# A graph network's convolutions: row products first, the constant row last in each bank, one product for both constants

## The chip, the cores and the metric

The kernel runs on one core of a Trainium2 chip, as one program. The metric is the device time of an execution in microseconds (us); lower is better. A core has five engines that work side by side: TensorE (PE) for matrix products, VectorE (DVE), ScalarE (ACT) and GpSimd (POOL) for work on tiles, SyncE (SP) for transfers. TensorE writes into PSUM, eight banks of 128 partitions x 512 fp32 numbers; the other tiles lie in SBUF.

## The reference, cut to what matters

Sixteen graphs (B) of 1024 nodes (N) with 128 features (D) pass four blocks: a graph network with dilated neighbourhoods, an attention, a graph attention and a graph convolution. The change is in the first block alone, after the dilation has thinned each adjacency:

```python
def _sage(x, adj, Wr, Wx, b, mf):
    deg = jnp.clip(jnp.sum(adj, axis=-1, keepdims=True), 1.0, None)
    agg = jnp.einsum('bij,bjd->bid', adj, x) / deg
    out = agg @ Wr + x @ Wx + b
    nrm = jnp.maximum(jnp.linalg.norm(out, axis=-1, keepdims=True), NORM_EPS)
    return out / nrm * mf[..., None]

def _bn(x, g, b):
    m = jnp.mean(x, axis=(0, 1))
    v = jnp.var(x, axis=(0, 1))
    return (x - m) * jax.lax.rsqrt(v + BN_EPS) * g + b

h1 = _bn(jax.nn.relu(_sage(x, adj_d, Wr1, Wx1, b1, mf)), g1, be1)
h2 = _bn(jax.nn.relu(_sage(h1, adj_d, Wr2, Wx2, b2, mf)), g2, be2)
h3 = _bn(jax.nn.relu(_sage(h2, adj_d, Wr3, Wx3, b3, mf)), g3, be3)
xc = jnp.concatenate([h1, h2, h3], axis=-1) * mf[..., None]
return (xc @ Wl + bl) * mf[..., None]
```

A batch normalization runs over all nodes of all graphs, so the statistics of a layer are complete only after its last graph.

## The kernel before, in words

The program has four stages: the dilation, the convolutions (`convolutions_plain`, in the profile from about 690 to 1611 us), the attentions, and a check whose fallback does not run. Only the convolutions matter here.

**Normalization folded into the next layer.** Instead of normalizing h, the kernel keeps the ReLU's output as it is. With `scale` and `shift` of the normalization, the next layer's weights become weight x scale per input feature (L1144), and the shift becomes a constant row: bias + shift @ Wx for every node, and shift @ Wr for those nodes that have a neighbour at all. `through` (L1129) makes both products of the shift with the unscaled weights; `row_parts` (L1007) splits the resulting 6 x 128 row into three bf16 parts, rows 0 to 2 for the first sum and 3 to 5 for the second. In L1143 the weights are scaled in place, after `through` has read them. `final` keeps the share of the last linear layer (`wl`, L1146 to L1148).

**One layer, per graph b.** A half graph (512 nodes) fills one PSUM bank, tile `o`, from a pool of four banks: two graphs. In it lie four blocks of 128 nodes. For a bank TensorE runs, in the text's order:

- L1087: the constant rows 0 to 2 for all four blocks at once, 3 rows of ones against a row that is repeated four times, 512 columns, bf16. It starts the bank's accumulation.
- L1091, layers 1 and 2: per block, the six rows of the constant against `has` (L1083). `has` is a 6 x 1024 bf16 tile made by VectorE from `rdeg`, one over the degree or zero, that is compared with `floor` per row: `floor` is 2 in rows 0 to 2, which no `rdeg` exceeds, so these rows of `has` are 0, and 0 in rows 3 to 5, so these are 1 where a node has neighbours. The tile has two buffers.
- L1093 and L1094: per block, the row products, aggT x Wr and hT x Wx, 128 x 128 fp32 (each appears as two records).

Then the chain of a graph: squares (L1099, ScalarE), sums over features (L1100, VectorE), a maximum (L1102), a power for the inverse root (L1045, GpSimd), eight scaled ReLUs (L1106, ScalarE). In layers 0 and 1 `neighbours` follows: transposes (L1029), copies to hT (L1030), a split of h into three bf16 parts (L676 to L679), 48 products g with the adjacency C (L1040), and the division by the degree into aggT (L1042). In layer 2 only transposes (L1114) and copies (L1115). Either way hT is spilled to memory (L1116) and its statistics are taken (L1118).

**The change of layer.** After the last graph: `bn_aggr` (L1120), the power for `scale` (L1123), `scale` times gamma (L1124), `shift` (L1126, L1127), the small products of `through`, `row` (L1141), `row_parts`, the scaling of both weights, the product of the shift with `wl`.

**Order.** Each engine works through its own queue in order. In this stage the queues are not in the text's order: a scheduler that knows each instruction's inputs and the free buffers fills waits of one graph with work of another. In the trace, for example, transposes of one graph stand between row products of another. In the attentions the order is written out by hand, with costs and due times; the diff doesn't touch it.

Of the kernel before, what the change touches and what calls it, by code (L numbers as in the profile page):

```python
# [6 lines left out]
F32 = mybir.dt.float32  # L7
# [5 lines left out]
ALU = mybir.AluOpType  # L13
# [4 lines left out]
B, N, D = 16, 1024, 128  # L18
P = 128
NB = N // P  # L20
H, HD = 4, 32
HN = N // 2
# [21 lines left out]
def flat(ap):  # L44
    return ap.rearrange("p a b -> p (a b)")
# [916 lines left out]
def convolutions_plain(tc, x, ident, ap, xp, h0, minus_half, kept, rdeg, spill, final, Wr, Wx, bias, gamma, beta, Wl, bl):  # L962
    nc = tc.nc
    with ExitStack() as ctx:
        cp = ctx.enter_context(tc.tile_pool(name="c_const", bufs=1))
# [9 lines left out]
        ones16 = cp.tile([3, P], BF16, name="ones16")  # L975
        nc.vector.memset(ones16, 1.0)

        floor = cp.tile([6, 1], F32, name="floor")
        nc.vector.reduce_sum(floor, ident[0:6, 0:3], axis=AX.X)
        nc.vector.tensor_scalar(floor, floor, 2.0, None, op0=ALU.mult)  # L980

        def matrix(w, name):
            t = cp.tile([P, D], F32, name=name)
            nc.sync.dma_start(t, w)
            return t

        def column(v, name):
            t = cp.tile([P, 1], F32, name=name)
            with nc.allow_non_contiguous_dma(reason="128 values, once"):
                nc.sync.dma_start(t, v[:, None])  # L990
            return t
# [8 lines left out]
        hT = [kp.tile([P, N], F32, name=f"hT{b}") for b in range(B)]  # L1000
        aggT = [kp.tile([P, N], F32, name=f"aggT{b}") for b in range(B)]
# [5 lines left out]
        def row_parts(rows, name):  # L1007

            left = small.tile([6, D], F32, name="left")
            nc.vector.tensor_copy(left, rows)  # L1010
            t = cp.tile([6, D], BF16, name=name)
            nc.vector.memset(t, 0.0)
            for k in range(3):
                part = small.tile([6, D], BF16, name="part")
                nc.vector.tensor_copy(part, left)
                nc.vector.tensor_tensor(left, left, part, op=ALU.subtract)
                nc.vector.scalar_tensor_tensor(t, part, pick[:, k:k + 1], t, op0=ALU.mult, op1=ALU.add)
            return t
# [25 lines left out]
        def rsqrt(out, v):  # L1044
            nc.gpsimd.tensor_tensor(out, v, minus_half[:, :v.shape[-1]], op=ALU.pow)  # L1045

        for b in range(B):
# [16 lines left out]
            if b == 1:  # L1064
                wr = [matrix(w, f"wr{i}") for i, w in enumerate(Wr)]
                wx = [matrix(w, f"wx{i}") for i, w in enumerate(Wx)]
# [4 lines left out]
                bet = [column(v, f"bet{i}") for i, v in enumerate(beta)]  # L1071
# [3 lines left out]
        wr_s, wx_s, constant = wr[0], wx[0], row_parts(b6[0], "const0")  # L1075
        for l in range(3):
            stats = kp.tile([P, 2 * B, 6], F32, name="stats")
            for b in range(B):
                if l:
                    rd6 = xp.tile([6, N], F32, name="xt")  # L1080
                    nc.sync.dma_start(rd6, rdeg[b][None, :].to_broadcast([6, N]))
                    has = w2.tile([6, N], BF16, name="has")
                    nc.vector.tensor_scalar(has, rd6, floor, None, op0=ALU.is_gt)  # L1083
                ps = []
                for hf in range(2):
                    t = pso.tile([P, HN], F32, name="o")
                    nc.tensor.matmul(t, ones16, constant[0:3, None, :].to_broadcast([3, 4, D]), start=True, stop=False)  # L1087
                    blocks = [(t[:, c * P:(c + 1) * P], slice((4 * hf + c) * P, (4 * hf + c + 1) * P)) for c in range(4)]
                    if l:
                        for o, rows in blocks:  # L1090
                            nc.tensor.matmul(o, has[:, rows], constant, start=False, stop=False)  # L1091
                    for o, rows in blocks:
                        nc.tensor.matmul(o, aggT[b][:, rows], wr_s, start=False, stop=False)  # L1093
                        nc.tensor.matmul(o, hT[b][:, rows], wx_s, start=False, stop=rows.stop % HN == 0)  # L1094
                    ps.append(t)
                nrm = small.tile([P, 2, NB], F32, name="nrm")
                for hf in range(2):
                    sq = w2.tile([P, 4, D], F32, name="sq")
                    nc.scalar.activation(flat(sq), ps[hf], AF.Square)  # L1099
                    nc.vector.reduce_sum(nrm[:, 0, 4 * hf:4 * hf + 4], sq, axis=AX.X)  # L1100

                nc.vector.tensor_scalar(nrm[:, 0, :], nrm[:, 0, :], 1e-24, None, op0=ALU.max)  # L1102
                rsqrt(nrm[:, 1, :], nrm[:, 0, :])
                h = w2.tile([P, NB, D], F32, name="h")
                for c in range(NB):
                    nc.scalar.activation(h[:, c, :], ps[c // 4][:, c % 4 * P:(c % 4 + 1) * P], AF.Relu,  # L1106
                                         scale=nrm[:, 1, c:c + 1])
                if l < 2:
                    neighbours(b, h)
                else:  # L1110
                    for hf in range(2):
                        t = pst.tile([P, HN], F32, name="t")
                        for c in range(4):
                            nc.tensor.transpose(t[:, c * P:(c + 1) * P], h[:, 4 * hf + c, :], ident)  # L1114
                        nc.scalar.copy(hT[b][:, hf * HN:(hf + 1) * HN], t)  # L1115
                nc.scalar.dma_start(spill[l, b], hT[b])  # L1116
                for hf in range(2):
                    nc.vector.bn_stats(stats[:, 2 * b + hf, :], hT[b][:, hf * HN:(hf + 1) * HN])  # L1118
            mv = small.tile([P, 2], F32, name="mv")
            nc.vector.bn_aggr(mv, stats.rearrange("p n s -> p (n s)"))  # L1120
            nc.vector.tensor_scalar(mv[:, 1:2], mv[:, 1:2], BN_EPS, None, op0=ALU.add)
            scale = cp.tile([P, 1], F32, name=f"scale{l}")
            rsqrt(scale, mv[:, 1:2])  # L1123
            nc.vector.tensor_tensor(scale, scale, gam[l], op=ALU.mult)  # L1124
            shift = cp.tile([P, 1], F32, name=f"shift{l}")
            nc.vector.tensor_tensor(shift, mv[:, 0:1], scale, op=ALU.mult)  # L1126
            nc.vector.tensor_tensor(shift, bet[l], shift, op=ALU.subtract)  # L1127

            def through(w, out, part):  # L1129
                six = small.tile([P, 6], F32, name="six")  # L1130
                nc.vector.memset(six, 0.0)
                nc.vector.tensor_copy(six[:, part], shift.to_broadcast([P, 3]))
                nc.tensor.matmul(out, six, w, start=part.start == 0, stop=part.stop == 6)

            if l < 2:
                wr_s, wx_s = wr[l + 1], wx[l + 1]
                ps = pst.tile([6, D], F32, name="t")
                through(wx_s, ps, slice(0, 3))
                through(wr_s, ps, slice(3, 6))
                row = small.tile([6, D], F32, name="row")  # L1140
                nc.vector.tensor_tensor(row, b6[l + 1], ps, op=ALU.add)  # L1141
                constant = row_parts(row, f"const{l + 1}")
                for w in (wr_s, wx_s):  # L1143
                    nc.vector.tensor_scalar(w, w, scale, None, op0=ALU.mult)  # L1144
            ps = pst.tile([3, D], F32, name="t")
            nc.tensor.matmul(ps, shift.to_broadcast([P, 3]), wl[l], start=True, stop=True)  # L1146
            nc.vector.tensor_tensor(last[0:3], last[0:3], ps, op=ALU.add)
            nc.vector.tensor_scalar(wl[l], wl[l], scale, None, op0=ALU.mult)  # L1148
# [671 lines left out]
```

## Time and profile before

| what | us |
|---|---|
| times of the runs | 4033.46, 4037.02, 4050.93 (median 4037.02) |
| the profiled execution | 4039.04 |
| its span in the profile | 4037.30 |
| TensorE busy over the span | 3474.4 (86%) |
| VectorE, ScalarE, GpSimd busy | 2527.9, 2401.7, 794.7 |
| layer 0 and the first neighbours' sums until its change of layer | from about 690 to 1160.5 |
| layer 1 | 1160.5 to 1458.5 |
| layer 2 and the last constants | 1458.5 to 1611.5 |
| L1087, 96 times | 384 ns median |
| L1091, 256 times | 214 ns median |

How to read it: the profile lists, per engine, each instruction with its start, its length, its line in the code, its output and inputs, and in brackets how long the engine was idle before it and whom it waited for. Neighbouring instructions of one kind are merged ("x2"). A matmul's record contains the depth of the pipeline, so what a product costs in a dense run is the distance from start to start. PEclk is the clock that was granted to TensorE as a share of full speed. The chain is the work that ended last, followed back from the end.

### The profile page before, as it was taken

To read this page: it belongs to the slowest core of one execution; us is meant where nothing else is said; L and a number is where in the kernel's file an instruction comes from. 1 tells how busy PE (TensorE), PEld (TensorE's weight loads), DVE (VectorE), ACT (ScalarE), POOL (GpSimd) and SP (SyncE) were. 2 spreads that over 40 slices of the span, in tenths; PEclk is the share of its full clock that TensorE was granted. 3 is DMA by queue.
4 is the path that set the end of the run, shared out by engine and by line. 5 is a ranking of instruction groups with operands and counts; after the bars stand their busy time and mean duration, and the time that the engine had idled before them with its cause. 6 is when DMAs were issued, how large, how long until landed. Compare 5 with 4: busy or idle time off the path is not lost.

```text
span 4037.3 us, 65855 instructions
## 1 busy us (share of the span) xinstructions
PE 3474.4 (86%) x26756; PEld 1998.6 (50%) x26756; DVE 2527.9 (63%) x4782; ACT 2401.7 (59%) x3961; POOL 794.7 (20%) x680
## 2 busy tenths in 40 slices
PE   4888887999999987778989988998898989989775
PEld 2556565445555566324444444444454444454333
DVE  4988774543344343328776876776777686777656
ACT  3778764543333334676667776767666767766540
POOL 7545521210000011101111112112111101211110
PEclk9999887999999998799999998999998999999887
DMA  9632223443333312411221221122122022111000
GB/s 106 40 21 16 14 97 116 165 159 126 125 111 121 108 68 85 142 37 53 74 79 43 64 79 60 51 74 74 43 69 80 26 74 79 58 59 48 27 17 17
DMA packets 182500, 293.21 MB, mean 73 GB/s; under 512 B 77468, under 2 KB 124456, under 8 KB 173992
## 3 DMA queue, kind: packets, MB, share of 16 engines
q1 hardware_dynamic: 91944, 221.69, 16.8%
q0 software_dynamic: 79728, 24.66, 7.5%
q10 hardware_dynamic: 10512, 42.54, 2.6%
q8 instruction: 212, 3.47, 0.4%
q14 instruction: 104, 0.85, 0.1%
HBM read 287.98 MB, written 51.19 MB: 84 GB/s over the span
## 4 chain that ended last, share of the span: by engine, by line
PE 58%; DVE 15%; ACT 7%; DMA 3%; issue 2%; POOL 2%; ACTq 0%; SPq 0%; POOLq 0%; DVEq 0%
PE g L1040 12%; PE acc L1444 9%; PE sum L1570 9%; PE t L1413 5%; PE sum L1624 4%; PE sum L1555 4%; DVE pm L1495 3%; PE o L1093 2%; PE sum L1357 2%; PE o L1094 2%; PE sum L1375 1%; ACT e L1421 1%; DVE rden L1450 1%; PE t L1029 1%; PE sum L1295 1%
## 5 line engine op out<-in xcount | busy, mean ns | idle before, releaser
L1421 ACT ACTIVATE e<-t 128x1024 f32<-128x1024 f32 x512 | 508.2, 1023 | 489.3 <-PE t L1413 472.9
L1495 DVE SCALAR_TENSOR_TENSOR pm<-dst,minus,A 128x1024 fp8e4<-128x1024 f32 x512 | 676.2, 1350 | 7.9 <-DMA dst<-scores 7.9
L1040 PE MATMUL g<-C,parts 128*128 128x512 fp8e4 x2304 | 521.3, 381 | 15.4 <-DVE aggT L1042 9.2
L1408 ACT ACTIVATE t<-A 128x2048 f32<-128x2048 fp8e4 x256 | 482.3, 1884 | 3.9 <-ACT dst L1475 0.3
L1570 PEld LDWEIGHTS <-pm 128*128 128x128 fp8e4 x4096 | 347.0, 98 | 187.1 <-issue 165.3
L1570 PE MATMUL sum<-parts,pm 128*128 128x198 bf16 x4096 | 400.3, 251 | 26.0 <-DVE pm L1495 16.3
L1444 PE MATMUL acc<-e,va 128*32 128x512 f32 x2048 | 330.5, 616 | 41.3 <-ACT e L1421 38.4
L1040 PEld LDWEIGHTS <-parts 128*128 128x128 bf16 x2304 | 223.1, 98 | 262.7 <-ACT parts L678 5.7
L1413 PE MATMUL t<-qT,kT 32*128 32x512 f32 x2048 | 307.7, 672 | 31.7 <-ACT t L1408 31.3
L1444 PE MATMUL acc<-e,ones_hd 128*32 128x512 f32 x2048 | 319.7, 601 | 0.0
L1573 DVE TENSOR_REDUCE pos<-sum 128x132 f32<-128x396 f32 x256 | 145.0, 566 | 204.0 <-PE sum L1570 203.4
L1555 PE MATMUL sum<-parts,A 128*128 128x396 bf16 x1024 | 210.8, 351 | 44.2 <-DVE parts L1547 23.9
L1042 DVE TENSOR_TENSOR aggT<-g,rdb 128x512 f32<-128x512 f32 x96 | 66.2, 690 | 269.2 <-PE g L1040 269.1
L1045 POOL TENSOR_TENSOR nrm<-nrm,minus_half 128x8 f32<-128x8 f32 x48 | 79.6, 1662 | 639.8 <-DVE nrm L1102 639.8
L1624 PE MATMUL sum<-A,gparts 128*128 128x512 fp8e4 x768 | 178.0, 385 | 24.9 <-ACT gparts L1607 17.6
L835 DVE TENSOR_TENSOR r<-ya,both 128x512 bf16<-128x512 f16 x184 | 140.2, 776 | 92.7 <-ACT ya L832 91.9
L1099 ACT ACTIVATE sq<-o 128x512 f32<-128x512 f32 x96 | 55.8, 599 | 226.1 <-PE o L1094 224.3
L1267 POOL TENSOR_TENSOR ln_st<-ln_st,minus_half 128x8 f32<-128x8 f32 x48 | 86.1, 1794 | 511.8 <-DVE ln_st L1265 377.1
L882 DVE SCALAR_TENSOR_TENSOR rows<-y,thirty,rows 128x1024 fp8e4<-128x1024 f16 x128 | 169.9, 1335 | 25.4 <-ACT y L874 24.6
L1555 PEld LDWEIGHTS <-A 128*128 128x128 fp8e4 x1024 | 94.5, 99 | 182.0 <-issue 104.1
L1106 ACT ACTIVATE h<-o,nrm 128x128 f32<-128x128 f32 x384 | 105.7, 384 | 116.9 <-POOL nrm L1045 113.7
L885 POOL TENSOR_TENSOR own<-rows,lower 128x256 bf16<-128x256 fp8e4 x128 | 109.5, 866 | 330.6 <-DVE rows L882 197.2
(287 smaller groups left out, 6937.7 us busy)
## 6 DMA issues: line engine op xcount, KB each, us to landing
a<-in_adj_dram SPq DMA_DIRECT2D x128, 512.0 KB
C<-kept SPq DMA_DIRECT2D x48, 1024.0 KB
dst<-scores SPq DMA_DIRECT2D x64, 512.0 KB
rdb<-rdeg SPq DMA_DIRECT2D x48, 512.0 KB
spill<-hT ACTq DMA_DIRECT2D x48, 512.0 KB
kept<-rows ACTq DMA_DIRECT2D x16, 1024.0 KB
h_a<-spill SPq DMA_DIRECT2D x64, 256.0 KB
hT_a<-spill SPq DMA_DIRECT2D x16, 512.0 KB
```

The lines of the kernel that those rows point to most:

```text
L835: nc.vector.tensor_tensor(r, ya, both[:, 1, :, None].to_broadcast([P, G, P]), op=ALU.is_equal)
L882: nc.vector.scalar_tensor_tensor(row, y16, hh[:, g:g + 1], row, op0=ALU.not_equal, op1=ALU.mult, saturate=False)
L1040: nc.tensor.matmul(ps, parts[:, k, j, :], C[:, j, cols], start=j == 0 and k == 0, stop=j == NB - 1 and k == 2)
L1408: nc.scalar.activation(s, A[b][:, k, None, cols].to_broadcast([P, H, HN]), AF.Copy, scale=16.0)
L1413: nc.tensor.matmul(s[:, hd], kT[r, k * P:(k + 1) * P], qT[r, cols], start=False, stop=True, skip_group_check=True)
L1421: nc.scalar.activation(es[:, hd:hd + 2], s[:, hd:hd + 2], AF.Exp, scale=SIGMA)
L1444: nc.tensor.matmul(ps[r], ones if one else va[:, k, r], es[:, hd], start=k == 0, stop=k == NB - 1)
L1495: nc.vector.scalar_tensor_tensor(pm[:, i, :], dst[hd], minus[:, i, hd:hd + 1], A[b][:, i, :], op0=ALU.is_ge, op1=ALU.mult, saturate=False)
L1555: nc.tensor.matmul(ps[:, :3 * H * W], A[b][:, i, j * P:(j + 1) * P], parts4[:, i, :, :, W:], start=i == 0, stop=i == NB - 1)
L1570: nc.tensor.matmul(ps[:, jj * 6 * W:(jj + 1) * 6 * W], pm[:, i, (j + jj) * P:(j + jj + 1) * P], flat(parts4[:, i, hd]), start=i == 0, stop ...
L1573: nc.vector.reduce_sum(pos[:, j:j + 2, hd, :], ps[:, :12 * W].rearrange("p (j s w) -> p j w s", j=2, s=3), axis=AX.X)
L1624: nc.tensor.matmul(ps, parts[:, k, m, :], A[b][:, m, cols], start=m == 0 and k == 0, stop=False)
```

## The change

Three edits in `convolutions_plain`:

- `floor` is -2 in rows 0 to 2 and stays 0 (as -0) in rows 3 to 5, so that `has` is 1 in rows 0 to 2 for every node. The product L1091 then adds both constants, and the wide product is left out in layers 1 and 2. In layer 0, which has no second constant, it stays.
- In a bank the row products come first, and the first of block 0 starts the accumulation; the constants come last.
- The scaled weights are new tiles (`scaled0`, `scaled1`), made right after `scale`, ahead of the shift, which moves into a small function `shifts`; `through` reads the unscaled weights.

```diff
-        nc.vector.tensor_scalar(floor, floor, 2.0, None, op0=ALU.mult)
+        nc.vector.tensor_scalar(floor, floor, -2.0, None, op0=ALU.mult)
...
                     t = pso.tile([P, HN], F32, name="o")
-                    nc.tensor.matmul(t, ones16, constant[0:3, None, :].to_broadcast([3, 4, D]), start=True, stop=False)
                     blocks = [(t[:, c * P:(c + 1) * P], slice((4 * hf + c) * P, (4 * hf + c + 1) * P)) for c in range(4)]
+                    for c, (o, rows) in enumerate(blocks):
+                        nc.tensor.matmul(o, aggT[b][:, rows], wr_s, start=c == 0, stop=False)
+                        nc.tensor.matmul(o, hT[b][:, rows], wx_s, start=False, stop=False)
                     if l:
                         for o, rows in blocks:
-                            nc.tensor.matmul(o, has[:, rows], constant, start=False, stop=False)
-                    for o, rows in blocks:
-                        nc.tensor.matmul(o, aggT[b][:, rows], wr_s, start=False, stop=False)
-                        nc.tensor.matmul(o, hT[b][:, rows], wx_s, start=False, stop=rows.stop % HN == 0)
+                            nc.tensor.matmul(o, has[:, rows], constant, start=False, stop=rows.stop % HN == 0)
+                    else:
+                        nc.tensor.matmul(t, ones16, constant[0:3, None, :].to_broadcast([3, 4, D]), start=False, stop=True)
                     ps.append(t)
...
             shift = cp.tile([P, 1], F32, name=f"shift{l}")
-            nc.vector.tensor_tensor(shift, mv[:, 0:1], scale, op=ALU.mult)
-            nc.vector.tensor_tensor(shift, bet[l], shift, op=ALU.subtract)
+
+            def shifts(l):
+                nc.vector.tensor_tensor(shift, mv[:, 0:1], scale, op=ALU.mult)
+                nc.vector.tensor_tensor(shift, bet[l], shift, op=ALU.subtract)
...
             if l < 2:
-                wr_s, wx_s = wr[l + 1], wx[l + 1]
+                wr_s, wx_s = [cp.tile([P, D], F32, name=f"scaled{k}") for k in range(2)]
+                nc.vector.tensor_scalar(wr_s, wr[l + 1], scale, None, op0=ALU.mult)
+                nc.vector.tensor_scalar(wx_s, wx[l + 1], scale, None, op0=ALU.mult)
+                shifts(l)
                 ps = pst.tile([6, D], F32, name="t")
-                through(wx_s, ps, slice(0, 3))
-                through(wr_s, ps, slice(3, 6))
+                through(wx[l + 1], ps, slice(0, 3))
+                through(wr[l + 1], ps, slice(3, 6))
                 row = small.tile([6, D], F32, name="row")
                 nc.vector.tensor_tensor(row, b6[l + 1], ps, op=ALU.add)
                 constant = row_parts(row, f"const{l + 1}")
-                for w in (wr_s, wx_s):
-                    nc.vector.tensor_scalar(w, w, scale, None, op0=ALU.mult)
+            else:
+                shifts(l)
```

## The prediction

> **What bounds the kernel now.** I read the page's chain first, to see who ends last, then the busy time by stretch, then the order of time at the two changes of layer, then the waits and VectorE's own order inside layer 2. Layers are counted l = 0, 1, 2 as in the code.
>
> ```profile
> PE 58%; DVE 15%; ACT 7%; DMA 3%; issue 2%; POOL 2%; ACTq 0%; SPq 0%; POOLq 0%; DVEq 0%
> ```
>
> ```profile
> core 0: us, PE busy (x) PEld busy (x) DVE busy (x) ACT busy (x) POOL busy (x), PEclk, DMA share, GB/s
> ...
> 1180.00:1390.00 210.00, 202.39 (x1152) 123.35 (x1151) 84.93 (x142) 75.15 (x183) 18.01 (x11) 0.98 0.32 115
> ...
> 1440.00:1590.00 150.00, 129.94 (x846) 100.44 (x845) 60.57 (x118) 67.14 (x183) 24.48 (x15) 0.90 0.14 54
> ```
>
> TensorE is the chain. In layer 1 (first line of figures: length of the stretch, then each engine's busy time) it is busy 202.4 of 210 us at clock 0.98: any product taken away there is time. Layer 2 is looser: 129.9 of 150, clock 0.90.
>
> The change of layer, here from 1 to 2, in order of time, TensorE's queue and then VectorE's:
>
> ```profile
> 1458.55 0.38 PE L1146 MATMUL t<-final,shift 128*3 128x128 f32 x2
> 1461.98 0.58 PE L1087 MATMUL o<-const,ones 3*128 3x512 bf16 x1 [3.04 <-DVE const L1017]
> 1462.36 0.63 PE L1091 MATMUL o<-const,has 6*128 6x128 bf16 x4
> ```
>
> ```profile
> 1458.83 0.26 DVE L1141 TENSOR_TENSOR row<-b,t 6x128 f32<-6x128 f32 x1
> 1459.02 0.27 DVE L1144 TENSOR_SCALAR wr<-wr,scale 128x128 f32<-128x128 f32 x1
> ...
> 1461.59 0.33 DVE L1017 SCALAR_TENSOR_TENSOR const<-part,pick,const 6x128 bf16<-6x128 bf16 x1
> ```
>
> TensorE has nothing to do for 3.04 us: the first product of the new layer is the constant row, and that is the last thing VectorE finishes. What follows runs at half speed: a pair of row products takes 0.43 us from start to start in the chain until about 1471, and 0.22 from there on. The stretch 1459 to 1474 has clock 0.66; the same place between layers 0 and 1 (wait 3.04 us at 1164.29) has 0.62 over 1161 to 1179.
>
> Steady work in layer 2, a piece of TensorE's queue, of VectorE's, and TensorE's again:
>
> ```profile
> 1553.73 0.38 PE L1087 MATMUL o<-const,ones 3*128 3x512 bf16 x1
> 1553.95 0.38 PE L1091 MATMUL o<-const,has 6*128 6x128 bf16 x4
> ```
>
> ```profile
> 1554.62 0.67 DVE L1100 TENSOR_REDUCE nrm<-sq 128x4 f32<-128x512 f32 x1
> 1556.90 0.74 DVE L1083 TENSOR_SCALAR has<-xt,floor 6x1024 bf16<-6x1024 f32 x1 [1.62 <-PE o L1091]
> 1557.57 1.26 DVE L1100 TENSOR_REDUCE nrm<-sq 128x4 f32<-128x512 f32 x2
> ```
>
> ```profile
> 1558.46 0.39 PE L1094 MATMUL o<-wx,hT 128*128 128x128 f32 x2
> 1561.17 1.10 PE L1114 MATMUL t<-ident,h 128*128 128x128 f32 x4 [2.33 <-ACT h L1106]
> ```
>
> Two things to see. The 512-wide constant product costs 0.22 us from its start to the next start (0.38 of its record is pipeline); cold it was 0.38 (1461.98 to 1462.36). And the second of the graph's two squares (L1099, ScalarE) starts at 1554.43 and is done at 1555.03, but its row sum starts only at 1557.57: in VectorE's queue it stands behind `has` of a later graph, which waits for TensorE's last reading of the tile it reuses (two buffers). TensorE pays with 2.33 us of waiting at the transposes, and a colder clock after it. The waits of 1464 to 1592 sum this up (total, times, longest):
>
> ```profile
> PE t L1114 <- ACT h L1106: 15.8, 9, 2.3
> DVE has L1083 <- PE o L1091: 29.2, 13, 5.8
> ```
>
> **What the Trainium skill says.** "TensorE: Matmul & The Clock Gate", part 1: the array falls to half clock after an idle window of about 3.4 us and needs as much busy time to come back. The trace agrees in kind: half speed after 3.04 us of idleness; but it stays there some 9 to 13 us, longer than the page's window. The table at the head of the same page gives VectorE a strict first-in-first-out queue; the blocked row sum shows it. "PSUM — Partial Sum Buffer", the four PSUM rules: the first matmul's flag clears the whole 2 KiB bank's marks, so one start in block 0 lets blocks 1 to 3 overwrite. No trace here shows that; I rely on it for the change doing what it says.
>
> **The change part by part.**
>
> *Wide constant product gone in layers 1 and 2* (`floor` now -2, so `has` is 1 in its first three rows and L1091 carries all six). 64 of 96 L1087 go, 0.22 us each warm. `has` is one operation of the same form (0.74 us). Each bank still changes from fp32 to bf16 and back once, so that cost (a pair before the change of type takes 0.32 instead of 0.22) stays. Layer 1, graphs 2 to 15: 28 x 0.22 = 6.2 us. But per two graphs TensorE waits once for ScalarE (1.52 us at 1393.34), and what is taken out between the bank that starts that chain and the wait only lengthens it: 7 x 0.22 = 1.5 back. I take **-4.6**; ends -7 (nothing given back) and 0.
>
> *Row products first, weights scaled ahead of the shift.* The scalings move to right after `scale` (1451.57 in layer 1's end), 0.27 us each, while TensorE has g products until 1458.1; VectorE's next dated work is the eviction at 1453.47, so they are free. If that cover were gone they would cost 2 x 0.2. Row products then need only what is long there; in TensorE's queue they follow the three small products (`through` twice, L1146), so they start at 1458.86. Eight blocks' pairs: bank A's rows end at 1460.7. Late next is the constant: `row` ends 1459.09, and the copy and three rounds of `row_parts` took 2.5 us where little stood between them (1608.24 to 1610.74), so 1461.6. TensorE waits there 0.9 us at most (nothing, if bank B's rows go ahead), then 0.32 for `has`, 1.9 for B's rows, 0.32: B is done at 1464.1 instead of 1471.4. Behind it the square, sum, power and ReLU chain is unchanged, so **-7** at this place. Ends: -3 (only the idle time goes, the clock falls all the same) and -8. Between layers 0 and 1 the same holds, but there graph 0's g products come next and must wait for the transposes, casts and subtractions (7.5 us today from 1177.5 to 1185, partly filled by the fourth bank, which will then be done early): the idle time may chill the clock again. I take **-6**, ends -3 and -8.
>
> *Order in the bank and the `has` queue (layer 2).* Constants now come last in the bank, so `has` of a later graph is free only after the rows too, 1.8 us later (less the wide products taken out). The orders on the engines are planned, not program order (transposes of one graph stand between rows of another), and are planned anew. With the release later, the row sums become ready first and should stand ahead of it in VectorE's queue; then `has` (0.74) falls into the time of the last square (0.60). The four blocked pairs of graphs (powers at 1524.67, 1541.89, 1559.08, 1576.24; 17.2 us apart) each lose 1557.57 - 1555.05 = 2.5: -10. The wide products add 8 pairs x 0.44 = -3.5 (half of the 4 x 0.22 in each, since the rest only lengthens a wait). A new plan is seldom perfect: I take **-12**. Ends: -21 (every graph at the early pace: powers at 1481.60, 1488.82, 1496.19 are 7.3 apart, less 0.44, is 6.8; 16 x 6.8 = 109 instead of some 130) and +5 (`has` stays ahead and waits 1.2 longer, four times).
>
> *Answers without a choice.* Layer 0 keeps its 32 wide products, moved last: nothing. Layer 2's end only calls `shifts` in the same place: nothing. Two new 128x128 tiles move later tiles of the pool by 1 KB per partition: taken as nothing, since the waits of this stage show engines and not room.
>
> Sum: -4.6 - 7 - 6 - 12 = -29.6. All of it lies on the chain, since the last stage begins with loads of what layer 2 spilled (first products at 1611). The profiled execution took 4039.04 us (span 4037.30 and 1.7 around it), so 4009.4; it lies 2.0 above the median shown, 4037.02, so as a median 4007.
>
> **Rivals.**
> 1. The queue clears everywhere: each term at its good end, -8 - 8 - 7 - 21 = -44, median 3993. For it: the pace early in layer 2 and a TensorE that needs only 4 x (8 x 0.22 + 0.32) + 16 x 0.11 = 10.1 us at full clock per two graphs. Against: ScalarE is busy 8.9 of 17.2 us and its chain is long.
> 2. `has` goes on blocking: boundaries and layer 1 as forecast, layer 2 +5: -12.6, median 4024. For it: VectorE takes it in order, and the wait already totals 29.2 us. Against: a later release is a reason to queue it later.
> 3. Slower: a new place for the constants. In layer 1 the bank that completes at 1401.4 does so just ahead of 44 g products (9.66 us), and its whole chain, square to casts at 1406.78 to 1407.97, hides under them. If its closing `has` products fell behind that run, some 7 us of the chain would lie open in each of 8 pairs: +56 - 29.6 = +26, median 4063. It decides from 3.7 us open per pair. For it: rows of one bank are already split around the run at 1414 to 1423. Against: `has` and constant are long ready, so nothing delays these products by data.
>
> **How the numbers follow.** Forecast 0.45, rival 1 0.20, rival 2 0.25, rival 3 0.10. 0.5%, about what a measurement tells from no change, is 20 us: below 4017 is faster. Of the forecast 0.38 lies there, of rival 2 0.05, all of rival 1: 0.63. Slower is rival 3: 0.10. Same 0.27. The range runs from inside rival 1 to past rival 2: 3988 to 4032.
>
> **What would show it.** L1087 x32 instead of x96; no wait on `const` above 1 us; clock over 0.85 in the first 15 us of layers 1 and 2; the second row sum within 0.3 us of its square in layer 2 and less than 8 us waited at L1114. I am wrong if `has` keeps standing ahead of the sums, or if layer 1's pairs grow beyond 35.1 us.

## The result and the profile after

| | median us, four runs each | range |
|---|---|---|
| before | 4038.14 | 4033.46 to 4050.93 |
| after | 3981.99 | 3977.22 to 3987.26 |

The ratio is 0.9856 (0.9842 to 0.9870), 56 us less: faster, as forecast, but by almost twice the forecast, and below the low end of the range (3988). The same kernel on another chip gave 0.9898 (0.9882 to 0.9915), 3989.59 against 4032.83: 43 us. By the medians the gain is thus some 43 to 56 us, and a single pair of profiles can't say more.

Where it went, by stage, from the two traces. A layer runs from the first small product of one change of layer (`through`) to that of the next, the last one to its last product with `shift`:

| stage, us | before | after | difference |
|---|---|---|---|
| to the end of layer 0 | 1160.4 | 1159.8 | -0.6 |
| change 0 to 1, to the first power of layer 1 | 15.0 | 7.4 | -7.6 |
| rest of layer 1 | 282.7 | 271.3 | -11.4 |
| change 1 to 2, to the first power of layer 2 | 15.0 | 7.0 | -8.0 |
| rest of layer 2 | 134.1 | 112.4 | -21.7 |
| from there to the end of the span | 2430.1 | 2423.8 | -6.3 |

The last line belongs to stages that the diff doesn't touch. Over all the profiles below it lies between 2417 and 2434 with no relation to the edits, and the first line between 1156 and 1169. So the -6.3 is not put down to anything, and what follows counts layers 1 and 2: -48.7 us.

The page's chain of after, shares of the span by engine:

```profile
PE 60%; DVE 20%; ACT 8%; DMA 5%; issue 3%; POOL 3%; ACTq 0%; SPq 0%; POOLq 0%; DVEq 0%
```

TensorE still leads. The shares of before added up to only 87%, these to 99%, so the higher numbers show a chain that was followed further, and not that an engine gained weight. The stretches say more. Layer 1 and layer 2 (to its last product into a bank `o`), before and then after; columns: stretch, its length, each engine's busy time, clock granted to TensorE, DMA share, GB/s:

```profile
1160.40:1458.10 297.70, 282.63 (x1575) 173.60 (x1574) 119.36 (x215) 103.95 (x256) 26.76 (x17) 0.95 0.30 110
1458.10:1593.14 135.04, 116.24 (x791) 95.34 (x790) 53.94 (x104) 62.98 (x171) 24.79 (x15) 0.89 0.15 58
```

```profile
1159.80:1438.60 278.80, 263.93 (x1548) 160.48 (x1548) 118.20 (x215) 102.32 (x256) 26.76 (x17) 0.98 0.33 117
1438.60:1546.51 107.91, 96.04 (x763) 82.66 (x762) 52.41 (x102) 65.18 (x179) 24.57 (x15) 0.97 0.18 72
```

TensorE's busy time falls by 18.7 and 20.2 us, far more than 64 products of 0.22 (14.1). The other part is the clock: 0.95 to 0.98 and 0.89 to 0.97. Busy time at half speed is counted in full, so busy alone hides what the clock costs. The length of both layers, up to the last product into a bank `o`, is therefore split into three: idle time of TensorE; time lost to the clock (half of the time in which TensorE is busy while the trace has its clock at one half); and the rest, the work at full speed.

| us over layers 1 and 2 | length | idle | lost to the clock | work at full speed |
|---|---|---|---|---|
| before | 432.7 | 33.9 | 28.7 | 370.2 |
| after | 386.7 | 26.7 | 6.6 | 353.3 |

The change takes out 17 us of work, 22 us of lost clock and 7 us of idleness.

In layers 1 and 2 of all these traces the clock is either full or half, and half speed comes in pieces of 3.41 us or a multiple of it. How many follow one and the same wait differs from profile to profile. TensorE right after its wait of some 3 us ahead of the constant of layer 2: in before, in e3_scale and in e6_merge_scale (two of the experiments below, which keep this wait, 2.88 us in both):

```profile
1461.26:1471.50 10.24, 9.52 (x43) 8.04 (x43) 1.96 (x5) 0.69 (x2) 0.00 (x0) 0.50 0.02 4
```

```profile
1458.81:1462.22 3.41, 3.41 (x19) 3.21 (x18) 0.00 (x0) 0.00 (x0) 0.00 (x0) 0.50 0.03 5
1462.22:1472.50 10.28, 8.75 (x66) 6.83 (x66) 3.15 (x6) 4.16 (x12) 1.65 (x1) 1.00 0.01 2
```

```profile
1455.50:1474.50 19.00, 15.73 (x131) 13.66 (x130) 6.91 (x12) 7.09 (x19) 3.62 (x2) 1.00 0.09 33
```

Before's profile is at the long end: half speed lasts 13.65 and 10.24 us at its two changes of layer. Over the twelve changes of layer that have this wait in all profiles, the first power comes 10.1 to 15.0 us after the change, with a median of 12.3; before has 15.0 twice. So some 3 us of each of the two differences at the changes of layer in the table by stage are the luck of before's profile.

TensorE's queue at the change from layer 1 to 2 in after:

```profile
1439.00 0.38 PE L1154 MATMUL t<-final,shift 128*3 128x128 f32 x2
1439.31 0.49 PE L1089 MATMUL o<-scaled,aggT 128*128 128x128 f32 x2
1439.63 0.39 PE L1090 MATMUL o<-scaled,hT 128*128 128x128 f32 x2
...
1442.63 0.61 PE L1093 MATMUL o<-const,has 6*128 6x128 bf16 x8
```

The row products start 0.31 us after the last small product, where TensorE had waited 3.04 us. Both banks' rows go ahead, and the constant, now one kind of product for all six rows, has 3.3 us more to be made: nothing waits for it. From the first pair on, a product follows the last one 0.22 us after it, which is the full clock.

VectorE's queue in layer 2 in after:

```profile
1493.56 1.25 DVE L1101 TENSOR_REDUCE nrm<-sq 128x4 f32<-128x512 f32 x2
1495.01 0.69 DVE L1101 TENSOR_REDUCE nrm<-sq 128x4 f32<-128x512 f32 x1 [0.20 <-ACT sq L1100]
1495.61 0.16 DVE L1103 TENSOR_SCALAR nrm<-nrm 128x8 f32<-128x8 f32 x1
1496.37 0.74 DVE L1083 TENSOR_SCALAR has<-xt,floor 6x1024 bf16<-6x1024 f32 x1 [0.60 <-PE o L1093]
```

The row sums here stand ahead of the blocked `has`, and wait only for their squares. That looks like the proof of the `has` step of the prediction; the experiments show that it isn't. And layer 0 keeps its wide products, as the instruction group shows (count, then shortest, median and longest in ns, and from when to when):

```profile
L1095 PE MATMUL o<-const,ones x32: 384/385/602, 796.2 to 1137.1; 3*128 3x512 bf16 x32
```

### The profile page after: what moved, and what is told of

It reads as the page before. It is cut to its first block, busy times and chain, and to the rows that moved or that the text cites. A ratio compares the mean times of both kernels' runs of the same rounds, so it can differ in the third digit from the quotient of the medians.

```text
span 3981.8 us, 65726 instructions
## 1 busy us (share of the span) xinstructions
PE 3429.2 (86%) x26692; PEld 1966.6 (49%) x26692; DVE 2528.4 (63%) x4782; ACT 2398.6 (60%) x3961; POOL 790.9 (20%) x680
## 4 chain that ended last, share of the span: by engine, by line
PE 60%; DVE 20%; ACT 8%; DMA 5%; issue 3%; POOL 3%; ACTq 0%; SPq 0%; POOLq 0%; DVEq 0%
PE g L1040 12%; PE acc L1452 10%; PE sum L1578 9%; PE t L1421 5%; PE sum L1632 4%; PE sum L1563 4%; DVE pm L1503 3%; DMA rows<-in_adj_dram 2%; DVE rows L882 2%; PE sum L1365 2%; PE o L1089 2%; DVE r L835 2%; PE o L1090 2%; ACT e L1429 1%; PE sum L1383 1%
## 5 line engine op out<-in xcount | busy, mean ns | idle before, releaser
L1632 PE MATMUL sum<-A,gparts 128*128 128x512 fp8e4 x768 | 176.3, 382 | 24.9 <-ACT gparts L1615 17.6
L872 PE MATMUL big<-tri,rows 128*128 128x256 fp8e4 (+3 forms) x896 | 175.6, 318 | 0.6 <-ACT y L874 0.4
```

The costliest lines, as they stand in the source:

```text
L872: nc.tensor.matmul(ps[:, k * P:], lhs, triF[:, :HN - k * P], start=k == 0, stop=k == 3)
L1632: nc.tensor.matmul(ps, parts[:, k, m, :], A[b][:, m, cols], start=m == 0 and k == 0, stop=False)
```

## The experiments

The change has three separable parts: **M**, the merged constant (no wide product in layers 1 and 2); **R**, rows first and constants last; **S**, the weights scaled early into new tiles. After is M, R and S together. Three theories stand in the expectations: W, that the wide products' width is what counts, so M is worth most; Q, that the queue order counts, R above all, because `has` blocks the row sums; C, that TensorE's stretches at half speed are a cost of their own, beside the waits that set them off.

| kernel | parts | median us | ratio to before (95%) | layers 1 and 2: idle, clock, work |
|---|---|---|---|---|
| e1_merge | M | 4008.40 | 0.9926 (0.9901 to 0.9951) | 29.4, 17.2, 356.2 |
| e2_rows | R | 4004.82 | 0.9920 (0.9889 to 0.9951) | 28.3, 6.8, 371.1 |
| e3_scale | S | 4038.00 | 1.0002 (0.9990 to 1.0014) | 35.0, 25.6, 369.7 |
| e4_rows_scale | R, S | 3999.12 | 0.9896 (0.9864 to 0.9928) | 24.9, 5.1, 370.7 |
| e6_merge_scale | M, S | 4014.31 | 0.9937 (0.9918 to 0.9956) | 32.3, 18.7, 355.5 |
| e5_merge_rows | M, R | 3977.20 | 0.9849 (0.9830 to 0.9868) | 24.3, 3.4, 353.3 |

**The merged constant alone.** The constants still open the bank:

```diff
-        nc.vector.tensor_scalar(floor, floor, 2.0, None, op0=ALU.mult)
+        nc.vector.tensor_scalar(floor, floor, -2.0, None, op0=ALU.mult)
...
-                    nc.tensor.matmul(t, ones16, constant[0:3, None, :].to_broadcast([3, 4, D]), start=True, stop=False)
...
+                        for c, (o, rows) in enumerate(blocks):
+                            nc.tensor.matmul(o, has[:, rows], constant, start=c == 0, stop=False)
+                    else:
+                        nc.tensor.matmul(t, ones16, constant[0:3, None, :].to_broadcast([3, 4, D]), start=True, stop=False)
```

> The kernel before with one edit: floor is -2 and the wide product is left out in layers 1 and 2, the six-row products come first in the bank and start it. Theory W (width: the gain over the forecast comes from the wide product, which costs more than its 0.22 us because it also lengthens waits and cold stretches): -35 us or more against before. Theory Q (queue: the gain comes from the constants being last, which takes 'has' out of the way of the row sums in VectorE's queue and leaves row products to fill waits): 64 x 0.22 = -14 us at most. Both: the 3.0 us wait for the constant stays at both changes of layer.

30 us less, which neither theory had. The work falls by 14.0, the 0.22 us a product of the prediction; lost clock falls by 11.5 and idleness by 4.5. From e3_scale to e6_merge_scale M takes out 14.2 us of work; where rows come first (e2_rows to e5_merge_rows, e4_rows_scale to after) 17.8 and 17.4, which is 0.27 to 0.28 a product; why it is more there stays open. The wait at the change of layer is still there between layers 0 and 1, as the waits of its layer 1 show (total, times, longest):

```profile
PE o L1090 <- DVE const L1017: 3.0, 1, 3.0
```

Between layers 1 and 2 it is gone, against both expectations: there the scheduler put the small products of the change ahead of the last graph's 44 g products, under which the constant is made. This, too, is part of the 30 us.

**Rows first alone.** The wide product stays, as the bank's last:

```diff
-                    nc.tensor.matmul(t, ones16, constant[0:3, None, :].to_broadcast([3, 4, D]), start=True, stop=False)
+                    for c, (o, rows) in enumerate(blocks):
+                        nc.tensor.matmul(o, aggT[b][:, rows], wr_s, start=c == 0, stop=False)
+                        nc.tensor.matmul(o, hT[b][:, rows], wx_s, start=False, stop=False)
...
+                    nc.tensor.matmul(t, ones16, constant[0:3, None, :].to_broadcast([3, 4, D]), start=False, stop=True)
```

> The kernel before with one edit: in each bank the row products come first, then the has products, then the wide product, which is kept. Weights are scaled where before scales them. Both theories: the two changes of layer gain 7 us each, less some 0.7 each for rows that wait for the late scaling: -14. Theory Q: layers 1 and 2 gain 20 more beside that, -34 in all. Theory W: nothing more, -14, and layer 2 keeps pairs of graphs of about 17 us.

34 us less, with nearly the same work (+0.9): it is 21.9 us of lost clock and 5.6 of idleness. Over all fifteen profiles the seven with rows first lose 3.4 to 9.5 us to the clock in layers 1 and 2, the eight with constants first 17.2 to 28.7, so this doesn't hang on one profile. Layers 1 and 2 of this kernel:

```profile
1158.40:1445.80 287.40, 273.60 (x1575) 164.00 (x1574) 119.16 (x215) 103.96 (x256) 26.74 (x17) 0.98 0.31 113
1445.80:1565.00 119.20, 104.34 (x799) 83.10 (x798) 53.75 (x105) 65.58 (x182) 24.57 (x15) 1.00 0.17 65
```

The clock in layer 2 is 1.00 where before has 0.89, although TensorE waits there 15 times. But only the first of these waits is 1.5 us; the others are at most 1.0 us, where before's in its layer 2 go up to 2.3:

```profile
PE t L1114 <- ACT h L1106: 14.1, 15, 1.5
```

Half of the gain is at the two changes of layer (first power after 8.1 us at both, instead of 15.0: -13.8), the other half in the steady work.

**Early scaling, alone and with each of the others.**

```diff
-                wr_s, wx_s = wr[l + 1], wx[l + 1]
+                wr_s, wx_s = [cp.tile([P, D], F32, name=f"scaled{k}") for k in range(2)]
+                nc.vector.tensor_scalar(wr_s, wr[l + 1], scale, None, op0=ALU.mult)
+                nc.vector.tensor_scalar(wx_s, wx[l + 1], scale, None, op0=ALU.mult)
+                shifts(l)
...
-                for w in (wr_s, wx_s):
-                    nc.vector.tensor_scalar(w, w, scale, None, op0=ALU.mult)
```

> The kernel before with one edit: the weights are scaled into new tiles right after scale, ahead of the shift. Both theories: within 2 us of before in every stage, since the constant stays first in the bank and is what TensorE waits for; the row_parts chain loses two fillers and may end 0.3 us earlier at each change of layer. The new tiles move later tiles by 1 KB: if that is what changes the attentions by -6 us, it shows here too.

> The changed kernel with the wide product put back as the last product of each bank in layers 1 and 2 (floor 2). Theory Q: 64 x 0.22 = +14 us against the changed kernel, so -42 against before. Theory W: +35 or more, so about -20 against before, with layer 2 back at some 8 us per graph.

> The changed kernel with the six-row products first in the bank, as before has them, merged and with the weights scaled early. Both theories: the wait of 3 us for the constant is back at both changes of layer, with a cold clock after it: +15 against the changed kernel. Theory W: that is all, -40 against before. Theory Q: another +20, so -20 against before.

S alone does nothing to the time: the constant row still comes first in the bank. (In its profile both changes of layer take 12.1 us instead of 15.0 all the same; the wait is nearly as long, but only one piece of 3.41 us at half speed follows it.) Added to R it gives 0.9896 instead of 0.9920, added to M 0.9937 instead of 0.9926: both within the intervals. Both e4_rows_scale (-39 us) and e6_merge_scale (-24) came out where Q put them (-42 and -20), and not W (-20 and -40).

**Merge and rows together, without the early scaling.** After, with these lines put back:

```diff
-                wr_s, wx_s = [cp.tile([P, D], F32, name=f"scaled{k}") for k in range(2)]
-                nc.vector.tensor_scalar(wr_s, wr[l + 1], scale, None, op0=ALU.mult)
-                nc.vector.tensor_scalar(wx_s, wx[l + 1], scale, None, op0=ALU.mult)
+                wr_s, wx_s = wr[l + 1], wx[l + 1]
...
+                for w in (wr_s, wx_s):
+                    nc.vector.tensor_scalar(w, w, scale, None, op0=ALU.mult)
```

> The changed kernel with the weights scaled in place and late, as before. Both theories: rows wait for the scaling some 0.7 us at each change of layer, so +1.5 us against the changed kernel, nothing elsewhere. If early scaling were what lets layer 2 run at 6.7 us per graph, it would show as +20.

M and R nearly add up: -30 and -34 alone, -60 together. Half or more of M's part is work, most of R's is lost clock. The version without S was expected to be 1.5 us slower than after; it came out some 5 us faster, though on another chip. So both ran again, on one chip:

> The changed kernel itself, for a direct comparison with e12 on the same chip: 3982 within 4.

> e5 again (merged, rows first, weights scaled in place and late). Its layers 1 and 2 took 392.0 us in the profile against 398.1 of the changed kernel, where one row product of the next layer stood between the last graph's sums and held them up by 2.6 us of waiting for the early scaled weight. If that is systematic: 4 to 8 us below e11; if the profiled executions differ by chance: the same.

After 3989.59, 0.9898 (0.9882 to 0.9915); without S 3975.73, 0.9866 (0.9849 to 0.9882). They are 14 us apart, where 4 to 8 were expected if the difference was systematic. The intervals just touch, but the traces agree with the medians: layer 1 is 278.8 and 281.2 us in after's two profiles, 272.2 in both of the version without S. The difference lies at the end of layer 1. TensorE's queue there, in after:

```profile
1419.06 2.29 PE L1029 MATMUL t<-ident,h 128*128 128x128 f32 x8 [3.84 <-ACT h L1107]
1422.54 1.03 PE L1040 MATMUL g<-C,parts 128*128 128x512 fp8e4 x2 [1.20 <-ACT parts L676]
1426.21 0.79 PE L1089 MATMUL o<-scaled,aggT 128*128 128x128 f32 x2 [2.63 <-DVE scaled L1142]
...
1428.08 10.55 PE L1040 MATMUL g<-C,parts 128*128 128x512 fp8e4 x44
```

and in the repeat of the version without S:

```profile
1417.53 1.04 PE L1029 MATMUL t<-ident,h 128*128 128x128 f32 x8
...
1420.88 9.67 PE L1040 MATMUL g<-C,parts 128*128 128x512 fp8e4 x44 [0.46 <-DVE parts L679]
...
1430.92 0.38 PE L1147 MATMUL t<-final,shift 128*3 128x128 f32 x2
1431.71 0.71 PE L1089 MATMUL o<-wr,aggT 128*128 128x128 f32 x4 [0.41 <-DVE wr L1145]
```

With S the first pair of row products of layer 2 needs only `scaled`, which comes early, and it was placed inside the g products of layer 1's last graph. `scaled` comes late all the same, TensorE takes its queue in order, and the 44 g products stand behind the pair: 2.63 us of waiting, the last of three waits that sum to 7.7 us. The clock had fallen before that: it is at half from 1419.63 to 1429.87, from just after the wait of 3.84 us, so that the run takes 10.55 us instead of 9.67. Late scaling costs one wait of 0.41 us instead. So e5_merge_rows is the best version here, ahead of both kernels.

Of the 6.5 to 9 us, only the 2.63 us are explained by S. The wait of 3.84 us comes from another grouping of the last graphs, and e1_merge, which has no S, shows the same grouping with a wait of 3.82 us, while e4_rows_scale, which has S, doesn't: its layer 1 is even 4 us shorter than that of e2_rows (283.2 and 287.4). Why the scheduler groups the graphs so is open.

**Is it `has` that blocks?** Three kernels test the prediction's reason in layer 2. The first is before with a third buffer for `has` (the unused tile `ones` makes the room); the second is e5_merge_rows with the same; the third makes `has` once, for graph 0, and uses it for all graphs, so that VectorE never has one in its queue in layer 2.

```diff
-                    has = w2.tile([6, N], BF16, name="has")
+                    has = w2.tile([6, N], BF16, name="has", bufs=3)
```

```diff
-                if l:
+                if l == 1 and b == 0:
...
-                    has = w2.tile([6, N], BF16, name="has")
+                    has = w2.tile([6, N], BF16, name="has", bufs=1)
```

> The kernel before with three buffers instead of two for has (an unused tile of ones gives the room). has then waits for a graph further back. Theory Q: VectorE's queue is no longer blocked in layer 2, its four slow pairs of graphs (17.2 us) fall to about 14.6: -10 us, and the waits for L1091 on VectorE nearly vanish. Theory W: the blocked queue is not what costs: within 3 us of before.

> e5 (merged, rows first, late scaling) with three buffers for has. If has still costs in the changed kernel's layer 2 (32.9 us of VectorE waiting on it, 11.9 us of TensorE waiting at the transposes), -5 us or more against e5; if it now stands only where VectorE has nothing else to do, within 3 us of e5.

> The kernel before with has made once, from graph 0's degrees, and used for all graphs and both layers; the other 31 makings, their transfers and their waits are left out. If has in VectorE's queue is what makes layer 2's pairs 17.2 us (theory Q), layer 2 falls from 149 us to 135 or less and the total by 14 us. If the pairs are bound by TensorE's work and its half-speed stretches (theory C, clock), layer 2 stays within 4 us.

Three buffers: 0.9979 (0.9969 to 0.9989) on before, and 0.9850 (0.9832 to 0.9867) on e5_merge_rows, the same as without. The first lies, with -7 us, between its two expectations. VectorE's wait for the tile remains there, against the expectation of Q; it may be that `has` is simply made one graph further ahead:

```profile
DVE has L1081 <- PE o L1089: 26.0, 12, 4.8
```

With `has` gone from the queue: 0.9977 (0.9968 to 0.9986), layer 2 after its first power 130.3 us instead of 134.1, and its pairs of graphs still take 15.4 to 19 us. TensorE's wait at the transposes in layer 2 is 12.0 us where before had 15.8, and the longest is 1.6 instead of 2.3:

```profile
PE t L1114 <- ACT h L1106: 12.0, 10, 1.6
```

From the first power of layer 2 to its last product into a bank, TensorE is idle for 4.9 us less than in before (10.9 and 15.8), but loses 3.5 us more to the clock (13.7 and 10.2), and the stretch is only 0.6 us shorter. So the blocked row sum is real and costs some 5 us of waiting, and the kernel gains 8 us by the medians; but it is not what makes the pairs slow.

**Is it the clock?** In one kernel, before gets 11 products without use ahead of the first wide product of layers 1 and 2, as cover for the 3.04 us; in the other, six ahead of each graph's transposes in layer 2. Both are extra work.

```diff
+                    if l and b == 0 and hf == 0:
+                        for _ in range(11):
+                            nc.tensor.matmul(t[:, :P], wr_s, wr_s, start=True, stop=True)
```

```diff
+                        if hf == 0:
+                            for _ in range(6):
+                                nc.tensor.matmul(t[:, :P], wr_s, wr_s, start=True, stop=True)
```

> The kernel before with 11 products of the scaled 128 x 128 weight with itself, into a bank that the wide product then starts anew, ahead of the first wide product of layers 1 and 2: they lie in the 3.0 us that TensorE waits for the constant and take 2.4 us. Nothing of the kernel's own work moves. Theory C (the half-speed stretch after the wait is a cost of its own): the time from the small products to the layer's first power falls from 15.0 us to about 10 at both changes of layer, with no pair of row products at 0.43 us; total -8 to -10. If the 15 us are only the wait and the work: unchanged.

> The kernel before with six products of the scaled weight with itself ahead of each graph's transposes in layer 2, in the bank that the transposes then overwrite: 16 x 6 x 0.22 = 21 us more work for TensorE, meant to lie where it waits for ScalarE. The scheduler plans the queue anew around them. Theory C (half-speed stretches after waits are the larger part of what layer 2 loses): the loss of 10.3 us to the clock in layer 2 falls below 3 and the layer takes no longer than before (149 us) in spite of the 21 us. If waits and clock matter little and TensorE is simply bound by its work: 149 + up to 21 = 165 us or more.

The first, TensorE's queue at the change from 1 to 2 and some 12 us later:

```profile
1465.26 2.72 PE L1089 MATMUL o<-wr 128*128 128x128 f32 x22 [0.41 <-DVE wr L1147]
1467.91 0.39 PE L1090 MATMUL o<-const,ones 3*128 3x512 bf16 x1
...
1468.78 0.39 PE L1097 MATMUL o<-wx,hT 128*128 128x128 f32 x2
1469.00 0.39 PE L1096 MATMUL o<-wr,aggT 128*128 128x128 f32 x2
...
1476.87 0.33 PE L1117 MATMUL t<-ident,h 128*128 128x128 f32 x1 [1.53 <-ACT h L1109]
...
1480.49 0.64 PE L1096 MATMUL o<-wr,aggT 128*128 128x128 f32 x2
1480.92 0.63 PE L1097 MATMUL o<-wx,hT 128*128 128x128 f32 x2
```

The row products start at once at full speed, 0.22 us apart, with the constant as late as in before: so idleness is needed for the half speed there. It isn't always enough, as e6_merge_scale shows above. The first power comes 10.7 us after the change instead of 15.0, at both changes. Yet the kernel's time is the same, 0.9996 (0.9985 to 1.0007): at 1480 the products are 0.43 apart again, the clock after it is 0.89, and the steady part of layer 2 gives back 3.1 us (layer 1: some 2). The other kernel became slower, 1.0050 (1.0034 to 1.0067), its layer 2 some 18 us longer (167 instead of 149) with the clock no higher:

```profile
1453.00:1619.00 166.00, 139.66 (x1000) 120.18 (x998) 59.64 (x112) 70.61 (x192) 26.41 (x17) 0.89 0.14 53
```

So useless products, placed like this, didn't buy the clock in the steady work: they are work in a stage that TensorE bounds, its waits at the transposes are still 1.5 us, and the half-speed stretches stay. Of the theories, neither W nor Q has the size of M; Q has the size of R, but not by its `has`; C fits R's part (its gain is lost clock for the most part), but C's own two tests gained nothing. Whether the low clock of before in steady layer 2 causes the slow order or follows from it, these runs don't separate.

## Why the prediction was right in direction and wrong in size

- **Changes of layer: right in mechanism, and in size with luck.** -6 and -7 forecast, -7.6 and -8.0 measured, by the mechanism given: no wait for the constant, and full clock behind it. The late-constant wait of 0.9 us didn't come, since both banks' rows went ahead, as the text allowed. But the forecast was read off the same profile of before whose half speed was unusually long; against the median of 12.3 us for a change with this wait, it would have been some -5 each.
- **Wide products in layer 1: mis-sized, at both of its terms.** "28 x 0.22 = 6.2" and "7 x 0.22 = 1.5 back" made -4.6; the rest of layer 1 fell by 11.4. The work there falls by 9.4, of which 1.0 only moved over to the change of layer, so that all 32 products of the layer are worth 8.3 (0.26 each). And nothing was given back: the wait at the transposes fell from 1.52 us to 1.12 for a pair of graphs, where the step had it grow. The clock, which this step left out, is another 4.9: before has seven waits of 1.52 us at the transposes in layer 1, four of them followed by 3.41 us at half speed; behind after's six waits of 1.12 us there is none. Idle time grew by 2.9, by the three waits at the end of after's layer 1.
- **Order and `has` in layer 2: this is the step that failed.** "The four blocked pairs of graphs (powers at 1524.67, 1541.89, 1559.08, 1576.24; 17.2 us apart) each lose 1557.57 - 1555.05 = 2.5: -10", with -3.5 for the wide products, made some -12; it was -21.7, about the good end (-21). TensorE's idle time up to the last product into a bank fell by 3.9 us only (15.8 to 11.9), not by 10. In its place came 6.8 us of lost clock (10.2 to 3.4), which the step put at nothing, 8.4 us of work, where it had 3.5, and 2.6 us after that last product. The term was read off a wait's own length. The colder clock behind it was seen and not priced, though a clock of 0.91 over the 118 us of the stretch says that some 10 us were lost. And the wait was put down to the neighbour in VectorE's queue, whose removal (e9_before_one_has) returns 4.9 us of idleness, loses 3.5 of them again to the clock, and leaves the pairs slow. That the whole came near the good end is luck: it is another sum.
- **Early scaling at no cost: wrong by 6 to 9 us of layer 1.** The step looked for what hides two operations on VectorE, and not for what else the scheduler may place differently once an input is early. Only 2.63 us of it are traced to that; the rest comes with the grouping of the last graphs, whose reason is open.
- **The rivals.** The first (everything at its good end, 3993) came nearest: its layer 2 is met to 0.7 us, but it had layer 1 at -7. `has` does go on waiting (32.9 us in layer 2), so the second was half right and of no consequence, since the sums shown stand ahead of it. The third did not happen: the closing constants stayed with their banks, and layer 1's pairs of graphs went from 35.95 to 33.53 us.
- **The signs.** Three of the five hold: L1087, now L1095, x32; no wait on `const`; no clock lost in the first 15 us of layers 1 and 2. The second row sum starts within 0.3 us of its square's end in nine of layer 2's 16 graphs only and mostly 0.6 us after it in the others (once 1.05), where before has 2.5 us in its four blocked graphs. Waits at the transposes in layer 2 are 11.9 us, not below 8.

The Trainium skill, "TensorE: Matmul & The Clock Gate", has in its section on a second failure mode of the gate that short idle times between groups of products, when they come often, make the clock swing between half and full. The trace of before agrees in kind: 0.91 in steady layer 2 with waits of at most 2.3 us. But the number of waits doesn't decide it here: e2_rows has 15 of them in layer 2, all but the first at most 1.0 us, and 1.00. Their length tells more, as the last section shows.

## What to carry to other kernels

Price a wait of TensorE by its length and by the half-speed stretch behind it: length times one minus the granted clock, read by stage, is a line of the sum like any other. Since that stretch differs from profile to profile behind the same wait, take it from several profiles, and not from the one that is to be beaten. An operation that stands ahead of a late one in a queue is a suspect and not yet the cause; remove it alone before giving it the whole delay. And where a scheduler orders the queues, making an input early also lets its consumer be placed early, ahead of work that was ready; look at the new order before counting the edit as free.

## What the runs showed that I had not expected

- What follows a wait of TensorE depends on its length, and on chance. Counted over layers 1 and 2 of all fifteen profiles (some of them of nearly the same order), for waits that began at full clock, half speed began in the wait or within 3.5 us of its end at 30 of 31 waits of 2.3 to 3.8 us, at 68 of 152 of 1.2 to 1.8 us, and at 5 of 140 of 0.2 to 1.2 us. Before's waits of 2.3 us in layer 2 lie in the first group, those of e9_before_one_has (1.1 to 1.6) mostly in the second, which goes with its clock not getting better, and those of e2_rows (at most 1.0 after the first) in the third.
- Half speed lasts 3.41 us or a multiple of it, also while TensorE is densely busy: after 3.04 us of idleness 13.65 and 10.24 us in before, after 2.88 us 3.41 us in e3_scale, and none at one of the two changes in e6_merge_scale.
- The change between fp32 and bf16 products is about 0.1 us (a pair ahead of it takes 0.32 instead of 0.22).
